# Spreading the attention weights one step earlier in a two-layer convolution block

## The chip, the cores and the metric

The kernel runs on one core of a Trainium2 chip. The metric is the device time of one execution in microseconds (us). Five engines of the core work side by side, each through its own queue in order: TensorE (PE, matrix products and transposes), VectorE (DVE, elementwise work and reductions), ScalarE (ACT, copies and activations), GpSimd (POOL, here it issues the gathers) and SyncE (SP, here it issues the plain transfers). Matrix products land in PSUM, from where ACT or DVE must fetch them before the place can be used again.

## The reference, cut to what matters

The input is 8 images of 256 channels and 64x64 positions, in float32. Two layers follow one another, each of the form x = x + layer(groupnorm(x)).

Layer 0 is attention over the 3x3 neighbourhood of each position, with 4 heads of 64 channels, together with a generated kernel:

```
q, k, v   = w_qkv @ x                        (1x1)
attn      = softmax over the 9 neighbours of q . k
kernel    = w_kg @ cat + b_kg                (9 values per head and position)
out       = w_proj @ (alpha * sum_k kernel * v_k + beta * sum_k attn * v_k)
```

Layer 1 is a modulated deformable 3x3 convolution: a small convolution gives 18 offsets and 9 masks per position, the image is sampled bilinearly at 9 moved places, and the samples are multiplied by a 256x256 matrix per tap and added.

## The kernel before, in words

**Tiling.** An image is cut into 8 chunks (`NC`) of 8 rows, that is 512 positions. 256 channels are 2 tiles of 128 partitions. In the attention, a chunk is seen as 8 tiles of 8x8 positions, each with a 10x10 neighbourhood of 100 keys (`NK`).

**Two streams.** The convolution of one image is woven into the attention of the next. The convolution is a loop over slots: one slot is one chunk and one of 9 taps, so 72 slots per image. A slot holds, on PE, 8 transposes of sampled rows (`pt`, line 816) and 8 passes of product matmuls (`po`, line 833). On ACT it holds two copies of the transposed rows (line 819) and four scalings of gathered rows (`s`, line 787), on DVE four times three multiply-adds (the sums, `s`, line 795), on POOL four gathers (`g`, line 771). The sums run 6 blocks of 128 positions ahead of the transposes, the scalings 8, the gathers 18; gathered rows have 10 buffers, and a slot has 4 blocks. The transposes use a PSUM pool of their own (`ps_t`), and so do the products (`ps_o`, one buffer, so that the first product of a chunk waits until DVE has added the chunk before to its residual, line 844).

**Front steps.** The attention of the next image, and after it the preparation of its convolution (table of rows, offsets, positions), is a generator, and each `yield` ends a step. The slot loop runs `transposes`, half of the look-ahead work, `product`, then a front step (a little over one per slot: there are 73 steps per image), then the other half of the look-ahead work. In a slot that ends a convolution chunk both halves and the final adds (`finished`) come before the front step. The order on PE, ACT, DVE and POOL is the order of the program text. The first image's front runs alone, before any slot.

**A chunk of attention** has seven steps. `a_` is the chunk itself, `d` the chunk before it, whose second half is worked off in between:

1. spread the weights of `d` (`spread_weights`), then `q` of `a_`
2. `k`
3. `products` q.k; `weighted(0)` of `d`
4. `logits`, second half of the value tiles of `d` (`keys(1)`), generated kernel, first part of the softmax
5. first half of `v`; `weighted(1)` of `d`; second part of the softmax; normalization of the next chunk
6. second half of `v`; first half of the output projection of `d` and its addition; `softmax_3`, which leaves the combined weights in `wts`
7. second half of the projection of `d`, its addition (`add`, line 544), statistics and storing of `d` (`second_stats`, line 548 and an SP transfer); `weights` (transposes of `wts`, line 467, copied to `wsb` by ACT, line 473); `keys(0)` (transposes of `v`, line 503, copied to `vk` by ACT, line 508)

After chunk 8 there are six more steps in which its second half is finished and the second group normalization is formed.

`spread_weights` does, per head, one matmul with a constant matrix of zeros and ones (line 480), which places the 9 weights of each position on its 100 keys, and one DVE product with a mask (line 488). Its four results live in the four buffers of `wk`.

**The shared PSUM pool.** All front steps take their PSUM from one pool in rotation, and a matmul waits until the user of the buffer four places earlier has been fetched:

```
ps_a = ctx.enter_context(tc.tile_pool(name="ps_a", bufs=4, space=PSUM))
```

In the kernel before, step 7 takes places for the projection, w and two vk; step 1 takes four for wk and two for q.

Of the kernel before, what the change touches and what calls it, by code (L numbers as in the profile page):

```python
# [19 lines left out]
NT = C // P  # L20
# [37 lines left out]
def preact_kernel(ctx: ExitStack, tc: tile.TileContext, a: dict, out: bass.AP):  # L58
# [161 lines left out]
    def normed(xt, gn, c):  # L220

        xn = xn2[c % 2]
        lo, hi = max(0, R * c - 1), min(H, R * c + R + 1)
        if c == 0:
            nc.vector.memset(xn[:, :, 0, :], 0.0)
        if c == NC - 1:
            nc.vector.memset(xn[:, :, R + 1, :], 0.0)
        o = lo - (R * c - 1)
        for ct in range(NT):
            nc.vector.tensor_scalar(  # L230
                xn[:, ct, o : o + hi - lo, 1 : W + 1],
                xt[:, ct, lo * W : hi * W].rearrange("p (r w) -> p r w", w=W),
                gn[:, 0, ct : ct + 1],
                gn[:, 1, ct : ct + 1],
                ALU.subtract,
                ALU.mult,
            )
        return xn
# [316 lines left out]
    def attention(b):  # L555

        xt = image
        gn = norm0[b]
        gn.means()
        stats = p2.tile([P, NT, NC, 6], F32, tag="stats", name=f"stats1_{b}")  # L560
        yield None
        gn = gn.ready()
        xn = normed(xt, gn, 0)
        yield None
        d = None
        for c in range(NC):
            a_ = Attention(b, c, xn, stats)
            if d:
                d.spread_weights()
            a_.q(0)  # L570
            a_.q(1)
            yield None
            a_.k(0)
            a_.k(1)
            yield None
            a_.products()
            if d:
                d.weighted(0)
            yield None
            a_.logits()  # L580
            if d:
                d.keys(1)
                d.carry_v()
            a_.generated()
            a_.softmax_1()
            a_.carry_k()
            yield None
            a_.v(0)
            if d:
                d.weighted(1)  # L590
            a_.turned()
            a_.softmax_2()
            if c + 1 < NC:
                xn = normed(xt, gn, c + 1)
            yield None
            a_.v(1)
            if d:
                d.add(0, d.project(0))
            a_.softmax_3()
            yield None  # L600
            if d:
                d.add(1, d.project(1))
                d.second_stats()
            a_.weights()
            a_.keys(0)
            yield None
            d = a_
        d.spread_weights()
        yield None
        d.weighted(0)  # L610
        d.keys(1)
        yield None
        d.weighted(1)
        yield None
        for m in range(NT):
            d.add(m, d.project(m))
        d.second_stats()
        gn = Norm(stats, f"1_{b}")
        yield None
        gn.means()  # L620
        yield None
        yield gn.ready()
# [129 lines left out]
    def fronts():  # L752
        for b in range(B):
            gn = None
            for got in attention(b):
                gn = got
                if gn is None:
                    yield
            yield
            yield from prepare(b, gn)  # L760
# [213 lines left out]
```

## Time and profile before

| what | value |
|---|---|
| time, median of 3 runs | 5197.73 us (5185.96 to 5206.68) |
| the profiled execution | 5546.8 us |
| its span, first to last instruction | 5545.0 us |
| mean granted PE clock in it | 0.939 of full speed |
| PE busy | 4874.6 us (88%) |
| DVE busy | 4170.6 us (75%) |
| POOL busy | 3287.5 us (59%) |
| ACT busy | 2368.6 us (43%) |

The profiled execution is longer than the unprofiled ones. A group of the profile names the line, the engine, the operation, what is written and read and how often; then busy time and mean nanoseconds of one; then the idle time of that engine just before these instructions, and what ended it. A wait reads as who waited, for whom, microseconds in total, how many times, and the longest. In the order of time a line begins with start and duration in microseconds; the idle time before it stands in brackets. A matmul in float32 appears as two passes, and the ends of matmuls are modelled: their distance from start to start is the better measure.

### The profile page before, as it was taken

What the parts mean: (1) busy time and instruction counts of PE and PEld (TensorE: products, weight loads), DVE (VectorE), ACT (ScalarE), POOL (GpSimd) and SP (SyncE); (2) the same over time, 40 slices, a digit from 0 to 9 for tenths busy, and PEclk for the clock granted to TensorE, in tenths of its full rate; (3) what the DMA queues carried; (4) which work ended last, traced back from release to release, by engine and by line L of the source; (5) the groups of instructions that cost most, each with busy time, mean ns of one, the idle gap of its engine ahead of it and who ended that gap; (6) DMA issues with size and microseconds to landing.
All of it is one profiled execution on the core that took longest, in us unless ns stands there. A gap on an engine that the chain in (4) does not pass through costs nothing. (4 is left out here: it accounts for less than half of the span.)

```text
span 5545.0 us, 79699 instructions
## 1 busy us (share of the span) xinstructions
PE 4874.6 (88%) x26592; PEld 2725.8 (49%) x26592; DVE 4170.6 (75%) x10071; ACT 2368.6 (43%) x5184; POOL 3287.5 (59%) x2310
## 2 busy tenths in 40 slices
PE   7979998899988998899988999989898899887677
PEld 4545554455544554455544555445554555443333
DVE  4567787788877787778878787878777777876666
ACT  2334444444444444444444444444444444443333
POOL 0036565666646666566656666566664666647776
PEclk9989999999999999999999999999999999998878
DMA  2067777777787777877787777877778677787777
GB/s 85 21 236 251 247 249 278 262 256 260 262 311 249 266 262 283 289 247 265 260 284 278 252 268 252 302 260 258 252 256 322 242 260 258 274 300 275 274 278 279
DMA packets 476840, 1422.60 MB, mean 257 GB/s; under 512 B 46910, under 2 KB 114750, under 8 KB 476300
## 3 DMA queue, kind: packets, MB, share of 16 engines
q0 software_dynamic: 331776, 1208.11, 61.9%
q1 hardware_dynamic: 141902, 204.27, 10.2%
q10 hardware_dynamic: 2750, 5.12, 0.3%
q8 instruction: 210, 3.44, 0.2%
q14 instruction: 202, 1.65, 0.1%
HBM read 1280.19 MB, written 137.13 MB: 256 GB/s over the span
## 5 line engine op out<-in xcount | busy, mean ns | idle before, releaser
L771 POOL DMA_INDIRECT g<-table,idx x2304 | 3284.9, 1426 | 2236.2 <-DVE s L795 585.5
L795 DVE SCALAR_TENSOR_TENSOR s<-g,wt,s 128x256 f32<-128x256 f32 x6912 | 2796.0, 478 | 566.5 <-ACT s L787 399.9
L833 PE MATMUL po<-vt,w_conv 128*128 128x512 f32 x4608 | 2187.8, 620 | 63.0 <-DVE r L844 37.4
L833 PEld LDWEIGHTS po<-vt,w_conv 128*128 128x128 f32 x4608 | 880.2, 202 | 965.9 <-issue 923.9
L787 ACT ACTIVATE s<-g,wt 128x256 f32<-128x256 f32 x2304 | 1068.5, 509 | 562.5 <-DMA g<-table,idx 464.7
L816 PE MATMUL pt<-ident,s 128*128 128x128 f32 x4608 | 725.0, 295 | 262.7 <-ACT vt L819 129.9
L816 PEld LDWEIGHTS pt<-ident,s 128*128 128x128 f32 x4608 | 547.4, 149 | 557.9 <-issue 184.4
L819 ACT COPY vt<-pt 128x512 f32<-128x512 f32 x1152 | 614.7, 584 | 423.3 <-PE pt L816 271.9
L281 PE MATMUL psq<-xn,w_qkvT 128*128 128x512 f32 x512 | 291.1, 720 | 113.2 <-DVE wk L488 108.4
L359 DVE TENSOR_TENSOR qk<-qk,near_k 128x400 f32<-128x400 f32 x256 | 129.8, 567 | 306.1 <-PE qk L351 165.2
L656 PE MATMUL om<-xn,w_off 128*32 128x512 f32 x2304 | 291.9, 604 | 7.7 <-DVE pos L689 7.4
L289 ACT COPY q<-psq 128x512 f32<-128x512 f32 x128 | 75.0, 586 | 483.7 <-PE psq L281 436.2
L313 PE MATMUL psk<-xn,w_qkvT 128*128 128x264 f32 (+1 forms) x1088 | 249.3, 382 | 10.9 <-ACT k L326 10.9
L313 PE MATMUL psv<-xn,w_qkvT 128*128 128x264 f32 (+1 forms) x1088 | 258.4, 382 | 0.0
L281 PEld LDWEIGHTS psq<-xn,w_qkvT 128*128 128x128 f32 x512 | 112.1, 229 | 290.6 <-DVE wk L488 161.1
L528 ACT COPY acc<-av 128x512 f32<-128x512 f32 x128 | 74.9, 585 | 414.4 <-PE av L521 320.8
L533 PE MATMUL proj<-acc,w_projT 128*128 128x512 f32 x512 | 239.8, 596 | 3.3 <-ACT s L787 2.7
L313 PEld LDWEIGHTS psv<-xn,w_qkvT 128*128 128x128 f32 x1088 | 199.9, 190 | 83.3 <-issue 46.4
L313 PEld LDWEIGHTS psk<-xn,w_qkvT 128*128 128x128 f32 x1088 | 202.3, 191 | 73.3 <-issue 20.2
L351 PE MATMUL qk<-k,q 64*64 64x100 f32 x4096 | 165.3, 260 | 78.5 <-issue 75.4
L351 PEld LDWEIGHTS qk<-k,q 64*64 64x64 f32 x4096 | 119.4, 136 | 155.0 <-issue 139.0
L335 ACT COPY v<-psv 128x320 f32<-128x320 f32 (+1 forms) x272 | 111.5, 417 | 187.3 <-PE psv L313 171.1
(89 smaller groups left out, 3375.0 us busy)
## 6 DMA issues: line engine op xcount, KB each, us to landing
table<-ts SPq DMA_DIRECT2D x384, 176.0 KB
g<-table,idx POOLq DMA_INDIRECT x2304
x<-in_x_dram SPq DMA_DIRECT2D x64, 512.0 KB
x<-x SPq DMA_DIRECT2D x64, 512.0 KB
r<-x SPq DMA_DIRECT2D x64, 512.0 KB
out_dram<-r SPq DMA_DIRECT2D x64, 512.0 KB
w_conv<-in_w_conv_dram ACTq DMA_DIRECT2D x1, 2304.0 KB
w_qkv<-in_w_qkv_dram ACTq DMA_DIRECT2D x2, 384.0 KB
```

Of the source, the lines that this page charges most:

```text
L281: nc.tensor.matmul(ps, w_qkvT[:, ct, m * P : (m + 1) * P], window(self.xn, ct, 4), start=(ct == 0), stop=(ct == NT - 1),)
L313: nc.tensor.matmul(ps[:, : (hi - lo) * WP], w_qkvT[:, ct, o : o + P], self.xn[:, ct, lo:hi, :], start=(ct == 0), stop=(ct == NT - 1),)
L351: nc.tensor.matmul(both[h][64 * t : 64 * t + 64, n : n + NK], self.qt[r, ct, o * T * T : (o + 1) * T * T], kt[r, ct, :, T * o : T * o + KT ...
L359: nc.vector.tensor_mul(qk[:, 2 * jj : 2 * jj + 2, :, h, :], both[h][:, : 4 * NK].rearrange("p (j c k) -> p j c k", j=2, c=NT), near_k.unsq ...
L533: nc.tensor.matmul(ps, w_projT[:, ct, m * P : (m + 1) * P], self.acc[:, ct].rearrange("p (t y x) -> p y t x", y=T, x=T), start=(ct == 0), ...
L656: nc.tensor.matmul(ps[32 * g : 32 * g + 32, :], w_off[:, ct, k, :], window(xn, ct, k), start=(n < 4), stop=(n >= KK * NT - 4),)
L771: nc.gpsimd.indirect_dma_start(out=g, out_offset=None, in_=tables[b % 2], in_offset=bass.IndirectOffsetOnAxis(ap=found[b, c][0][:, j, k : ...
L787: nc.scalar.activation(s, g[:, 0:C], AF.Copy, scale=w[:, 0:1])
L795: nc.vector.scalar_tensor_tensor(s, g[:, q * C : (q + 1) * C], w[:, q : q + 1], s, ALU.mult, ALU.add)
L816: nc.tensor.transpose(pt[ct][:, j, :], s[:, ct * P : (ct + 1) * P], ident)
L819: nc.scalar.copy(v[:, ct, :], pt[ct].rearrange("p b n -> p (b n)"))
L833: nc.tensor.matmul(po[:, m, :], w_conv[:, ct, k, m * P : (m + 1) * P], v[:, ct, :], start=(k == 0 and ct == 0), stop=(k == KK - 1 and ct = ...
```

## The change

The spreading of a chunk's weights moves from step 1 of the next chunk to step 7 of its own chunk. In step 7 `weights` and `keys(0)` move ahead of the projection's second half; then come the projection, its addition, the spreading, and the statistics of the chunk before. Behind chunk 8 the step that held only its spreading is gone, and the two halves of the last projection are two steps in place of one, so that the number of steps is the same.

```diff
         for c in range(NC):
             a_ = Attention(b, c, xn, stats)
-            if d:
-                d.spread_weights()
             a_.q(0)
             a_.q(1)
             yield None
...
             a_.softmax_3()
             yield None
+            a_.weights()
+            a_.keys(0)
             if d:
                 d.add(1, d.project(1))
+            a_.spread_weights()
+            if d:
                 d.second_stats()
-            a_.weights()
-            a_.keys(0)
             yield None
             d = a_
-        d.spread_weights()
-        yield None
         d.weighted(0)
         d.keys(1)
         yield None
         d.weighted(1)
         yield None
-        for m in range(NT):
-            d.add(m, d.project(m))
+        d.add(0, d.project(0))
+        yield None
+        d.add(1, d.project(1))
         d.second_stats()
         gn = Norm(stats, f"1_{b}")
         yield None
```

## The prediction

> **What bounds the kernel now.** I read the page first, then the waits of TensorE in one image (2373 to 2806 us, the fifth image's seven chunk boundaries), then busy time by stretch, then the order of time around one boundary.
>
> ```profile
> PE 4874.6 (88%) x26592; PEld 2725.8 (49%) x26592; DVE 4170.6 (75%) x10071; ACT 2368.6 (43%) x5184; POOL 3287.5 (59%) x2310
> ...
> L281 PE MATMUL psq<-xn,w_qkvT 128*128 128x512 f32 x512 | 291.1, 720 | 113.2 <-DVE wk L488 108.4
> ```
>
> TensorE (PE) is busiest. One group, the q matmuls, has 113.2 us of idle time before it, 108.4 of it ended by VectorE's (DVE's) wk products. PE's waits in the fifth image, with total, times and longest:
>
> ```profile
> PE psq L281 <- DVE wk L488: 16.2, 7, 5.8
> PE qk L351 <- issue: 7.4, 14, 1.0
> PE po L833 <- DVE r L844: 3.1, 1, 3.1
> PE pt L816 <- DVE s L795: 1.6, 6, 0.5
> ```
>
> This wait is the largest and comes once per boundary. Busy time by stretch (stretch, length, PE, weight loads, DVE, ACT, POOL, clock, DMA); three run from the projection of step 7 to the transposes after the next chunk's q, then a whole image, then the last image's convolution alone:
>
> ```profile
> 2559.60:2574.50 14.90, 12.49 (x49) 6.01 (x48) 14.90 (x35) 4.75 (x10) 11.25 (x6) 1.00 0.76 257
> 2498.10:2514.80 16.70, 14.22 (x50) 6.62 (x49) 15.56 (x36) 4.82 (x10) 13.36 (x8) 0.90 0.80 271
> 2434.20:2454.50 20.30, 14.31 (x49) 6.79 (x48) 19.00 (x44) 5.76 (x12) 16.06 (x8) 0.83 0.77 254
> 2373.00:2806.00 433.00, 401.48 (x2267) 232.55 (x2268) 343.75 (x795) 196.72 (x440) 278.34 (x195) 0.96 0.75 260
> 5010.00:5540.00 530.00, 382.82 (x1111) 191.15 (x1109) 341.70 (x834) 194.79 (x410) 376.46 (x268) 0.83 0.74 282
> ```
>
> Over the image PE is busy 401.48 of 433.00 us and DVE 343.75: PE bounds it. But inside the first stretch DVE is busy without a break: here DVE bounds, and PE waits on it. The order of time there:
>
> ```profile
> 2558.64 0.37 DVE L455 SCALAR_TENSOR_TENSOR wts<-lt,beta,kb 128x144 f32<-128x144 f32 x1
> 2558.93 4.83 DVE L795 SCALAR_TENSOR_TENSOR s<-g,wt,s 128x256 f32<-128x256 f32 x12
> 2559.59 1.88 PE L533 MATMUL proj<-acc,w_projT 128*128 128x512 f32 x4
> 2561.31 0.60 PE L467 MATMUL w<-ident,wts 128*128 128x128 f32 x4
> 2561.75 1.04 PE L503 MATMUL vk<-ident,v 128*100 128x128 f32 x8
> 2562.62 0.60 PE L816 MATMUL pt<-ident,s 128*128 128x128 f32 x4
> 2563.68 0.68 DVE L544 TENSOR_TENSOR x<-proj,x 128x512 f32<-128x512 f32 x1
> 2564.09 3.60 PE L833 MATMUL po<-vt,w_conv 128*128 128x512 f32 x8
> 2565.47 4.83 DVE L795 SCALAR_TENSOR_TENSOR s<-g,wt,s 128x256 f32<-128x256 f32 x12
> 2567.62 1.12 PE L480 MATMUL wk<-wsb,spread 9*100 9x512 f32 x8
> 2570.21 2.48 DVE L488 TENSOR_TENSOR wk<-wk,near 100x512 f32<-100x512 f32 x4
> 2570.95 3.71 PE L281 MATMUL psq<-xn,w_qkvT 128*128 128x512 f32 x8 [2.21 <-DVE wk L488]
> 2574.50 1.04 PE L816 MATMUL pt<-ident,s 128*128 128x128 f32 x8
> ```
>
> The four wk matmuls take all four buffers of the PSUM pool. DVE reaches their products only after twelve sums (4.83 us), and q, behind them on PE, needs the buffers back.
>
> [...] while q waits 2.21 us, transposes behind it, which need no PSUM of this pool, wait too. [...] with the same work and the same 2.21 us wait, the second stretch has clock 0.90 and lasts 16.70, not 14.90.
>
> **The change part by part.** No instruction is added or removed per chunk. The four wk matmuls (eight passes in the trace) and their four DVE products move one step up; in step 7 the order becomes w, vk, projection, add, wk, statistics.
>
> *A usual boundary (4 of 7 per image), timed from 2559.59.* PE distances from the start times above: projection 1.72, w 0.44, vk 0.87, one wk 1.12/4 = 0.28, q 3.55. After: w needs wts, which ends at 2559.01, 0.58 early; the projection no longer covers that, and nothing is lost while the margin lasts (up to 1.72 if it is gone). wsb's ACT copy is covered by vk and the projection. So w, vk, projection and three wk end at 0.44 + 0.87 + 1.72 + 0.84 = 3.87. The fourth wk takes the projection's buffer, so it waits for the add: this wait is new. The add is behind the sums, so it starts at 4.08 as now and ends at 4.76; with the fourth wk PE goes on at about 5.1. Queued behind it are the convolution's transposes, 0.9 (they are stretched to 1.47 by sums now; by 5.1 those are done), products 3.5, q 3.55: the next transposes start at 13.1 against 14.91 now. DVE: add until 4.7, wk products 2.4, statistics 1.2, twelve sums 4.75: 13.0, just in time for those transposes; the six sums (2.46) that now stand behind wk inside the stretch fall after it, where DVE has a 0.67 us wait today. Gain 1.8 at full clock. Slowed boundaries last 16.7 to 16.9; [...] I leave a third of the present loss. The four last 16.3 on average here, 15.4 in the calmer seventh image; 15.85 less 13.5 (13.1 plus 0.4) is 2.35, times 4 is 9.4 per image. Ends: 1.8 x 4 = 7.2 and 3 x 4 = 12.
>
> *The boundary at 2434 (one per image).* A convolution chunk is finished in the slot of q, so DVE does 18 sums and two adds of 0.64 before wk, and PE waits 5.78. After: add 4.7, wk 7.1, statistics 8.3, sums 15.4, adds 16.6; the convolution's next product, which needs those adds, starts at 16.7 against 21.2 now. Gain 4.5.
>
> *The first boundary* (no projection, wait 0.76): wk follows vk at 1.3 and hides DVE's lateness for the next transposes; 10.5 against 11.5, gain 1.0. *The sixth* (chunk finished in step 7, the add only at 7.7): the fourth wk waits until 8.5, transposes follow, and the end is where it was: 0, or a loss of 1 if the clock cools longer.
>
> *Sum:* 9.4 + 4.5 + 1.0 = 14.9 per image, times 7 interleaved images: 104.
>
> *Elsewhere.* The eighth chunk's step 7 grows by 1.5 (PE's next product at 6.0 for 4.5), the spread step behind it disappears (1.1), and the last add before the second normalization stands alone, about 1 less DVE time ahead of its matmul: taken as +0.6 per image, 4 in all, bounds -10 and +15. In the first image's front, with nothing interleaved, wk's products wait for the add: 0.4 x 7 = 3 lost. SP's store of the block, issued behind the statistics, goes 2.4 later; its reader is in a later image. SP is passed by nothing else. POOL: the twelve sums come later and free gather buffers later; below.
>
> Total 104 + 4 - 3 = 105. The profiled execution is 5546.8 us, 1.8 of it outside the span, so 5442. The unprofiled median, 5197.7, is 349 lower; the waits are made of DVE durations, which I take as unchanged, so I subtract the same 105: **5092 us**. Scaling by 5197.7/5546.8 would give 98 and 5099.
>
> **The rivals.** *DVE takes it all back.* It is full in the usual stretch. If all its present work must still fit ahead of the transposes, only its idle time there can be won. Over the seven stretches of the image that is 116.8 - 108.4 = 8.4, less 3.4 of the sixth: 5 per image, 35 in all: 5163. Against it: the last six sums are not needed by those transposes.
>
> *The gathers turn it slower.* The twelve sums end at 13.0 in place of 10.7 and free gather buffers 2.4 late; if POOL issues at once, data, ACT's scaling and DVE's sums come as much later. Fully exposed, 2.4 x 56 steps (8 per image) = 134, less 105: 5227. It decides once the gathers' slack is so small that over 105/56 = 1.9 per step comes through. For it: at 2443 and 2447 ACT does wait 2.58 and 3.71 for gathers. Against it: ACT's wait for gathers between 2446 and 2746 is small,
>
> ```profile
> ACT s L787 <- DMA g<-table,idx: 7.0, 3, 3.7
> ```
>
> and POOL issues the gather that reuses the first of these buffers at 2571.41, 3.5 after the first six sums ended (2567.9): it is behind anyway.
>
> *The clock gains more.* If no boundary cools any more, and c. 1 us more per boundary falls away after it: 12 + 5.5 + 1 + 1 per image, times 7, is 137; with the tail's +15, 152: 5046. For it: four of seven stretches here are slowed.
>
> *Nothing moves:* if PE's idle time only shifts to the new wait for the add, 5198. Against it: that wait is 0.9, not 2.2.
>
> **How the numbers follow.** Forecast 0.60 (own range 5060 to 5130), DVE 0.17, clock 0.10, slower 0.08, nothing 0.05. A measurement of this kernel tells about 0.5% (26 us) from no change. Faster: 0.60 + 0.10 + 0.13 of DVE's 0.17 = 0.83; same: 0.05 + 0.04 = 0.09; slower 0.08. The range takes in clock and most of DVE: 5035 to 5175.
>
> **What would show it.** Right: q's wait for wk near 0; a wait of about 0.9 at the fourth wk ended by the add; no wait of w for wts over 0.5; usual stretches near 13.1 to 13.5; the boundary that waits 5.78 now shorter by over 4 with a wait of the product for the two adds in its place; clock in these stretches nearer 1.00. Wrong: w waiting for wts, transposes waiting for sums by over 1 us, or ACT's wait for gathers (464.7 in all now) up by 50 or more.

## The result, and the profile after

The changed kernel takes 5218.51 us (median of 20 runs, 5200.66 to 5230.65) where the kernel before takes 5199.17 (20 runs, 5185.96 to 5219.39). The ratio is 1.0029, with a 95% interval of 1.0017 to 1.0042: 0.3% slower, which is less than the 0.5% that the prediction named as the least it could tell from no change. The forecast was 5092.

One thing must be known to read the numbers: both kernels take longer on some chips than on others, the kernel before some 5200 us on one kind and 5530 to 5560 on the other, and the profile shown ahead of the prediction (5546.8 us) fits the second. ("Kind of chip" is only a name for these two levels: each chip is on record in one session, so the cause may lie in the session and not in the chip.) The profile after (5205.54 us, span 5203.8) is of the first kind. So it is set beside a second profile of the kernel before on a chip of that kind (5206.58 us, span 5204.8); times are compared only within one kind, and kernels by their ratio to the kernel before on the same chip.

The page of the changed kernel, busy time by engine and the group of the q matmuls (line numbers from 567 on are one lower than before):

```profile
PE 4778.5 (92%) x26592; PEld 2668.8 (51%) x26592; DVE 4173.8 (80%) x10071; ACT 2379.9 (46%) x5184; POOL 3148.3 (60%) x2310
...
L281 PE MATMUL psq<-xn,w_qkvT 128*128 128x512 f32 x512 | 236.3, 604 | 1.6 <-DVE xn L230 1.6
```

The wait that the prediction set out to remove is gone: q had 113.2 us of idle time before it, and has 1.6. PE's waits in the fifth image (2376 to 2806 us) of the changed kernel, with total, times and longest:

```profile
PE wk L480 <- DVE x L544: 6.6, 6, 3.5
PE po L832 <- DVE r L843: 5.9, 3, 2.1
PE pt L815 <- ACT vt L818: 3.8, 1, 3.8
PE av L521 <- DVE qk L359: 3.6, 2, 2.0
```

In the place of q's wait stands the fourth wk's for the addition. The wait in the last line, which was 1.5 us in the fifth image of the first profile before, is not at a boundary. Busy time by stretch at the same boundaries, first of the kernel before (its second profile; stretch, length, PE, weight loads, DVE, ACT, POOL, clock, DMA; the first two end at the transposes behind q, the third at the product behind them):

```profile
2475.84:2490.75 14.91, 12.49 (x50) 6.02 (x49) 14.91 (x35) 4.75 (x10) 11.25 (x6) 1.00 0.75 250
2415.67:2432.26 16.59, 14.18 (x49) 6.62 (x48) 15.46 (x36) 4.75 (x10) 12.63 (x7) 0.90 0.78 257
2352.24:2374.54 22.30, 16.31 (x57) 7.99 (x56) 19.05 (x44) 6.35 (x13) 17.72 (x9) 0.77 0.77 259
```

and then of the changed kernel:

```profile
2478.36:2492.03 13.67, 13.08 (x50) 6.31 (x49) 13.67 (x32) 4.82 (x10) 8.27 (x5) 1.00 0.80 265
2419.43:2434.78 15.35, 14.76 (x50) 7.37 (x48) 15.35 (x36) 4.82 (x10) 9.95 (x5) 0.89 0.71 236
2359.79:2376.51 16.72, 14.11 (x57) 7.10 (x56) 16.72 (x39) 8.18 (x17) 11.02 (x6) 1.00 0.66 230
```

A usual boundary at full clock went from 14.91 to 13.67, a slowed one (clock 0.90 and 0.89) from 16.59 to 15.35, the long one from 22.30 to 16.72. Each of the three is shorter, and the time is not. Where the gain went can be read from a division of the whole span, worked out from the traces. A boundary runs from the first matmul of step 7 to the first product after the next chunk's q; seven boundaries and the seven stretches behind them make up most of an image; the values per image are means over the third to the eighth image.

| us | before, second profile | after, first profile | after, second profile |
|---|---|---|---|
| first slot begins (first image's front alone) | 359.7 | 382.9 | 385.5 |
| seven boundaries | 121.5 | 111.7 | 112.2 |
| seven stretches between them | 290.9 | 299.3 | 297.7 |
| step 7 of chunk 8 to the second normalization | 41.8 | 40.6 | 41.5 |
| from there to the next image's first boundary | 178.5 | 177.0 | 177.2 |
| slots of the seven interleaved images, sum | 4436.0 | 4413.5 | 4417.6 |
| the last image's convolution | 409.0 | 407.3 | 415.1 |

The boundaries gain 9.5 us per image, 66 in seven images. The stretches between them, in which the change touches no instruction, lose 7.6 (mean of the two profiles), 53 in seven. The first image's front, once per execution, loses 24.5. The first row and the last two add up to the span, which is 1.0 us shorter in the first and 13.4 us longer in the second of these profiles than before.

### The profile page after: what moved, and what is told of

Its sections match the earlier page's. It is cut to its first block, busy times and chain, and to the rows that moved or that the text cites. A ratio compares the mean times of both kernels' runs of the same rounds, so it can differ in the third digit from the quotient of the medians.

```text
span 5203.8 us, 79622 instructions
## 1 busy us (share of the span) xinstructions
PE 4778.5 (92%) x26592; PEld 2668.8 (51%) x26592; DVE 4173.8 (80%) x10071; ACT 2379.9 (46%) x5184; POOL 3148.3 (60%) x2310
## 5 line engine op out<-in xcount | busy, mean ns | idle before, releaser
L770 POOL DMA_INDIRECT g<-table,idx x2304 | 3145.7, 1365 | 2033.3 <-DVE s L794 757.7
L786 ACT ACTIVATE s<-g,wt 128x256 f32<-128x256 f32 x2304 | 1089.4, 510 | 637.3 <-DMA g<-table,idx 567.6
L832 PEld LDWEIGHTS po<-vt,w_conv 128*128 128x128 f32 x4608 | 866.9, 198 | 960.2 <-issue 882.5
L815 PE MATMUL pt<-ident,s 128*128 128x128 f32 x4608 | 685.1, 286 | 106.9 <-DVE s L794 82.1
L815 PEld LDWEIGHTS pt<-ident,s 128*128 128x128 f32 x4608 | 527.0, 145 | 425.0 <-issue 173.6
L281 PE MATMUL psq<-xn,w_qkvT 128*128 128x512 f32 x512 | 236.3, 604 | 1.6 <-DVE xn L230 1.6
L544 DVE TENSOR_TENSOR x<-proj,x 128x512 f32<-128x512 f32 x128 | 87.9, 687 | 133.2 <-PE proj L533 133.2
L480 PE MATMUL wk<-wsb,spread 9*100 9x512 f32 x512 | 146.5, 641 | 51.0 <-DVE x L544 50.5
L326 ACT COPY k<-psk 128x264 f32<-128x264 f32 (+1 forms) x272 | 97.4, 372 | 196.2 <-PE psk L313 196.1
```

What stands on the lines that cost most here:

```text
L281: nc.tensor.matmul(ps, w_qkvT[:, ct, m * P : (m + 1) * P], window(self.xn, ct, 4), start=(ct == 0), stop=(ct == NT - 1),)
L480: nc.tensor.matmul(ps[:NK], spread[32 * h : 32 * h + KK], self.wsb[32 * h : 32 * h + KK], start=True, stop=True,)
L770: nc.gpsimd.indirect_dma_start(out=g, out_offset=None, in_=tables[b % 2], in_offset=bass.IndirectOffsetOnAxis(ap=found[b, c][0][:, j, k : ...
L786: nc.scalar.activation(s, g[:, 0:C], AF.Copy, scale=w[:, 0:1])
L815: nc.tensor.transpose(pt[ct][:, j, :], s[:, ct * P : (ct + 1) * P], ident)
L832: nc.tensor.matmul(po[:, m, :], w_conv[:, ct, k, m * P : (m + 1) * P], v[:, ct, :], start=(k == 0 and ct == 0), stop=(k == KK - 1 and ct = ...
```

## The experiments

**A second profile of each kernel, on one chip.** No edit.

> The kernel before, unchanged, profiled a second time. The first profile of it lasted 5546.8 us, 6.7% over its own median of 5199; the profile of the changed kernel lasted 5205.5. If the first profile was disturbed (slower transfers from outside the kernel), this one lasts 5180 to 5230 and its last image, the convolution alone, takes about 410 us as in the changed kernel in place of 544; then the waits that the forecast was built on are to be read again from here. If profiling itself costs the kernel before 6%, it lasts 5500 or more again.

> The changed kernel, unchanged, profiled again beside the kernel before on one chip: 5200 to 5230. Theory A (the boundaries between chunks gain what was forecast and another stage gives it back): its seven boundaries per image sum to 8 to 15 us less than those of the kernel before, and the tail of each image's attention, its preparation or the last image is longer by as much. Theory B (the boundaries of an undisturbed kernel before had less to give): the boundaries differ by under 4 us per image and every stage by little.

Measured: 5206.58 and 5219.98 us, the table's first and third columns. Both losses named above are in the second profile of the changed kernel as they are in the first. The theory is from here on: the boundary works, and two other places pay for it. The rivals are that the numbers of the boundary are wrong, or that a single cause makes both losses.

**The first image's front in its old order.** In the first image nothing is interleaved, so the chain of work is bare. The order of time in one step 7 of it, the kernel before:

```profile
139.88 3.60 PE L533 MATMUL proj<-acc,w_projT 128*128 128x512 f32 x8
144.95 0.37 DVE L455 SCALAR_TENSOR_TENSOR wts<-lt,beta,kb 128x144 f32<-128x144 f32 x1
145.47 0.63 PE L467 MATMUL w<-ident,wts 128*128 128x128 f32 x4 [1.99 <-DVE wts L455]
148.78 3.71 PE L281 MATMUL psq<-xn,w_qkvT 128*128 128x512 f32 x8
```

and the changed kernel:

```profile
147.91 0.37 DVE L455 SCALAR_TENSOR_TENSOR wts<-lt,beta,kb 128x144 f32<-128x144 f32 x1
148.33 0.67 PE L467 MATMUL w<-ident,wts 128*128 128x128 f32 x4 [3.62 <-DVE wts L455]
148.83 1.88 PE L503 MATMUL vk<-ident,v 128*100 128x128 f32 x8
150.50 2.76 PE L533 MATMUL proj<-acc,w_projT 128*128 128x512 f32 x4
155.08 3.71 PE L281 MATMUL psq<-xn,w_qkvT 128*128 128x512 f32 x8
```

Before, both halves of the projection (eight passes) ran while the softmax was not yet ready, in time in which PE had nothing else; w then waited 1.99. After, PE waits 3.62, and the second half runs behind w and vk, on the path from `wts` to the next chunk's q. After that wait PE is slowed as well: from 148.9 to 152.2 the granted clock is 0.50, vk takes 1.88 and four projection passes 2.76, where they take 1.04 and 1.88 at full clock. From the start of `wts` to q it is 7.17 us for 3.83, and a chunk's period rises from 27.16 to 30.5 (from the third chunk on). The experiment gives the first image alone the old order:

```diff
         for c in range(NC):
             a_ = Attention(b, c, xn, stats)
+            if d and b == 0:
+                d.spread_weights()
...
-            a_.weights()
-            a_.keys(0)
+            if b > 0:
+                a_.weights()
+                a_.keys(0)
             if d:
                 d.add(1, d.project(1))
-            a_.spread_weights()
+            if b > 0:
+                a_.spread_weights()
             if d:
                 d.second_stats()
+            if b == 0:
+                a_.weights()
+                a_.keys(0)
             yield None
             d = a_
+        if b == 0:
+            d.spread_weights()
```

> The changed kernel, with the first image's attention, which runs alone, in the order of the kernel before; the seven interleaved images keep the change. If the first image lost by the order of step 7 (the projection no longer runs while PE waits for the softmax weights, 1.6 us a chunk, and the clock cools in the longer wait), the first slot starts at 360 us in place of 384 and the time is 20 to 26 lower: 5190 to 5200. If the later start came from something else (the start of the program), 5210 to 5225.

Measured: 5192.99 us (5183.8 to 5216.81), ratio to the kernel before 0.9994 (0.9981 to 1.0007). The first slot begins at 360.4 us, as before the change, and the median falls by 25.5 us (by the two ratios it is 0.35%, some 18 us), near the 24.5 that the table showed. This loss is separate from the other, which is left as it was: seven stretches between boundaries take 296.8 us per image in it.

**What fills the stretches between the boundaries.** In the changed kernel a stretch with a loss looks like this, in the order of time behind one boundary:

```profile
4428.69 11.95 DVE L794 SCALAR_TENSOR_TENSOR s<-g,wt,s 128x256 f32<-128x256 f32 x30
4431.48 9.97 POOL L770 DMA_INDIRECT g<-table,idx  x1 [2.35 <-DVE s L794]
...
4444.56 0.51 ACT L786 ACTIVATE s<-g,wt 128x256 f32<-128x256 f32 x1 [2.03 <-DMA g<-table,idx]
4445.10 0.48 DVE L794 SCALAR_TENSOR_TENSOR s<-g,wt,s 128x256 f32<-128x256 f32 x1 [4.47 <-ACT s L786]
...
4449.80 2.01 DVE L359 TENSOR_TENSOR qk<-qk,near_k 128x400 f32<-128x400 f32 x4
4450.42 1.01 PEld L521 LDWEIGHTS av<-wk,vk 100*64 100x64 f32 x32 [2.63 <-DVE qk L359]
4450.42 1.15 PE L521 MATMUL av<-wk,vk 100*64 100x64 f32 x32 [2.44 <-DVE qk L359]
```

VectorE does thirty corner sums without a break, 11.95 us. GpSimd starts a gather 2.8 us into them and is not done with it until 9.97 us later, 0.8 after the last sum, where an ordinary gather takes 0.94. The next gathers are late by as much; so are ACT's scalings, DVE's sums, DVE's product for q.k that is queued behind these, and PE. Elsewhere it is k's copy on ACT that stands behind a scaling, and PE's q.k that waits for it: 21.9 us, five times, in the whole profile. Before the change the wk products, whose second operand lies in PSUM, stood between twelve of these sums and the eighteen behind them, and in places a wait of DVE for ACT; 4 unbroken runs of thirty sums are in that trace, and 21 after the change (20 in its second profile); none is longer. In both kernels most gathers of over 1.5 us end 0.8 us after a run of sums (357 of 360 before, 304 of 312 after), so gathers were held before, too, and the time lost in long ones is even a little less after (898 us for 931). But more of them are held very long: over 8 us last 14 before and 22 after (23 in the second profile), and it is one of these behind which PE waits above. To begin inside a run is not enough: of 853 gathers of the changed kernel that begin inside a run with over 1 us of it still to go, 300 are held.

The hold is of some 23 sums, from 4431.48 to the end of the run at 4440.64, and not of one of 0.48 us.

Four experiments take this apart. The first two put a memset of one column (59 ns, 1152 times) ahead of each group of sums, in the changed kernel and in the kernel before. It runs while a sum does, so that DVE's busy time grows by only 9 us (4182.6 for 4173.8 in the changed kernel):

```diff
         work = [sums[n] for n in (i, i + 1) if n in sums]
+        if work:
+            nc.vector.memset(pause, 0.0)
         for q in range(1, 4):
```

> The changed kernel with one more VectorE instruction in front of every group of six (or three) sums: it sets one column of a tile that nothing reads. Theory A (a gather that POOL issues while VectorE runs sums without a break is held until the run ends; the change joined 12 and 18 sums to 30): runs of sums are 6 long at most, no gather lasts over 3.5 us, ACT's wait for gathers falls from 568 us to under 450, the stretches between the boundaries go back from 298 to about 291 us per image; less some 0.1 us for each of 1152 groups where VectorE bounds, 5160 to 5200 us. Theory B (VectorE is full and simply late, whatever POOL does): the added instructions make it later still, 5225 to 5300.

> The kernel before with the same added instruction. Theory A: it too has gathers held by runs of 12 and 18 sums (931 us over the 0.94 us of a free one); they fall below 300 us, but its transposes seldom wait for gathers, so the time moves little: 5180 to 5215. Theory B: slower by the added work, 5210 to 5280.

Measured on one chip: 5073.03 us (5069.23 to 5077.91), ratio 0.9747 (0.9721 to 0.9774), for the changed kernel; 5103.71 (5102.34 to 5104.84), ratio 0.9809 (0.9782 to 0.9835), for the kernel before. An instruction added on the second busiest engine made both kernels faster, and by more than the theory had it (5160 to 5200 and 5180 to 5215). In the changed kernel with the memset, the order of time at a place like the one above:

```profile
4328.72 0.06 DVE L795 MEMSET pause<- 128x1 f32 x1
4329.11 2.46 DVE L798 SCALAR_TENSOR_TENSOR s<-g,wt,s 128x256 f32<-128x256 f32 x6
4331.11 0.06 DVE L795 MEMSET pause<- 128x1 f32 x1
4331.49 2.46 DVE L798 SCALAR_TENSOR_TENSOR s<-g,wt,s 128x256 f32<-128x256 f32 x6
4331.50 0.94 POOL L772 DMA_INDIRECT g<-table,idx  x1 [4.01 <-DVE pause L795]
```

The gather again starts 2.8 us behind the first sum (at 4328.71) and just after the start of a sum, and takes 0.94. No gather of the 2304 lasts over 1.25 us. The gathers' group in the changed kernel,

```profile
L770 POOL DMA_INDIRECT g<-table,idx x2304 | 3145.7, 1365 | 2033.3 <-DVE s L794 757.7 <-DVE pi L691 359.3 <-ACT s L786 272.4
```

and with the memset:

```profile
L772 POOL DMA_INDIRECT g<-table,idx x2304 | 2329.0, 1011 | 2721.1 <-DVE pause L795 913.3 <-ACT s L788 367.5 <-DVE gt L697 367.2
```

(busy time and mean ns; then the idle time, which is no loss by itself). ACT's waits for gathers go from this in the changed kernel

```profile
ACT s L786 <- DMA g<-table,idx: 567.6, 473, 9.0
```

to this with the memset:

```profile
ACT s L788 <- DMA g<-table,idx: 238.9, 271, 5.6
```

With the hold taken away from both kernels, the loss between the boundaries is gone, and the change gains again:

| us | before + memset | after + memset |
|---|---|---|
| first slot begins | 358.9 | 390.5 |
| seven boundaries, per image | 124.5 | 112.4 |
| seven stretches between them, per image | 290.9 | 291.3 |
| step 7 of chunk 8 to the next image's first boundary | 205.2 | 208.2 |
| slots of the seven interleaved images, sum | 4346.9 | 4289.1 |
| the last image's convolution | 395.9 | 396.4 |

The interleaved images are 57.8 us shorter with the change, of which the first image's front takes 31.6 back. Much of what the memset itself brings lies elsewhere: from step 7 of chunk 8 to the next image's first boundary it takes the kernel before from 220 to 205 us per image and the changed kernel from 218 to 208. In the kernel before it takes nothing from the stretches, and its boundaries are 3 us per image longer with it.

The third puts the statistics of the chunk before, which the change had moved to the end of step 7, at the start of the next step, in front of q:

```diff
-        d = None
+        d = old = None
         for c in range(NC):
             a_ = Attention(b, c, xn, stats)
+            if old:
+                old.second_stats()
             a_.q(0)
...
             a_.spread_weights()
-            if d:
-                d.second_stats()
             yield None
-            d = a_
+            old, d = d, a_
+        old.second_stats()
         d.weighted(0)
```

> The changed kernel with the two statistics of a chunk moved from step 7 to the beginning of the next step 1, so that they stand between 12 and 18 sums: no work added or taken away. Theory A: no run of 30 sums is left at the boundaries, the longest gathers there last 5 to 7 us in place of 10, the stretches between boundaries lose 3 to 6 of their added 7 us per image: 5175 to 5205. Theory B: VectorE has as much to do in the same time, 5210 to 5225.

Measured: 5182.0 us (5171.6 to 5190.52), ratio 0.9956 (0.9941 to 0.9972). The statistics (1.27 us) now stand between the twelve sums and the eighteen behind them: 3 unbroken runs of thirty in place of 21, 9 gathers of over 8 us in place of 22, and the stretches between boundaries take 292.8 us per image in place of 298.5. No work is added or taken away in it, and the memset's other effects play no part; but the order of DVE's work changes too, and what that is worth by itself is seen further down ("The mends together"). The first image's loss stays (387.6).

The fourth asks whether the break must be an instruction without two SBUF inputs (Theory A1), as the memset and the wk products with their operand in PSUM are, or can be any small one (A2). It puts an addition of two small SBUF tiles (two columns) in the memset's place:

```diff
+        if work:
+            nc.vector.tensor_add(pause, pair[0], pair[1])
```

> The changed kernel with another small instruction at the same places: a sum of two two-column tiles, both in SBUF, in place of the one-column set without an input. Theory A1 [...]: gathers stay held, some still last 10 us, ACT's wait for gathers stays over 450 us, 5200 to 5260 us. Theory A2 (any small instruction that interrupts the sums lets POOL in, by its short time or by a pause of the engine): as with the set, no gather over 3.5 us and 5070 to 5110 us.

Measured on a chip of the second kind: 5375.41 us (5367.76 to 5390.54), ratio 0.9732 (0.9701 to 0.9763). No gather is over 2.3 us long, but 510 are over 1.5. Of the gathers that begin inside a group of six with over 1 us of it still to go, 209 of 786 are held, all until 0.8 us after the end of their group. So a hold ends where the unbroken run of the large sums ends, and a short instruction with two SBUF inputs ends it, too. The memset does more: on a chip of that kind none of 842 gathers that begin in the same way inside a group is held, so that it keeps holds from beginning and does not only end them. Why is not settled by this. Nor is which gathers are caught: in the changed kernel 298 of the 300 held ones begin within 52 ns behind the start of a sum, with the addition none of the 209.

**The projection ahead of the weights.** Step 7 with the projection first, as in the kernel before, and the spreading still in step 7:

```diff
-            a_.weights()
-            a_.keys(0)
             if d:
                 d.add(1, d.project(1))
+            a_.weights()
+            a_.keys(0)
             a_.spread_weights()
```

> The changed kernel with the projection and its addition ahead of the weights' transposes in step 7, as the kernel before had them; the spreading stays in step 7. The projection covers the wait for the softmax weights again in the first image: the first slot starts at 360 to 368 us in place of 384. But the first of the four spreading matmuls now takes the projection's PSUM buffer, so all four wait for the addition, not only the last: some 0.8 us more at the usual boundaries, 20 to 35 us in all. Together 5190 to 5230 us.

Measured on a chip of the second kind: 5665.75 us (5652.36 to 5672.21), ratio 1.0240 (1.0209 to 1.0271). The first slot begins at 358.0 us, so the first image's loss comes from the place of the projection and not from that of the spreading. The boundaries are as short as in the changed kernel on such a chip (112.5 us per image for 113.2), so the 0.8 us that each was to lose did not come. But it was 2.4% slower than the kernel before, and nothing in the theory so far made so much.

**The mends together.** The memset with the old order of the first image; then these two with the statistics moved as above for all images but the first:

> The changed kernel with both mends together: the added one-column instruction ahead of each group of sums (alone 5073 us), and the first image in the old order (alone 25 us less than the changed kernel). If the two losses are separate, they add: 5040 to 5055 us, first slot at 360 to 365 us.

> The kernel with both mends, and the statistics moved from step 7 to the next step 1 in the interleaved images. With the runs of sums broken in any case, the move can only bring the sums 1.2 us earlier after step 7 and the statistics later: no gain from gathers is left, -1.2 us at the boundaries where VectorE ends last (the one at which a chunk of the convolution is finished), so 0 to 15 us less than both mends alone. If the gain of 36 us that this move brought alone came from VectorE's order and not from the gathers, it brings 25 to 40 here too.

Measured on a chip of the second kind, beside a kernel before of 5527.94 us: 5268.24 (5252.59 to 5291.71), ratio 0.9534 (0.9507 to 0.9561), and 5205.58 (5204.82 to 5223.9), ratio 0.9429 (0.9403 to 0.9454). The first slots begin at 361.3 and 359.4 us, as expected. But moving the statistics took off 63 us, more than the 0 to 15 of the theory and than the 25 to 40 of its rival, and no gather is held in either kernel. 57 of them are in the interleaved images, 17 in the stretches between the boundaries (306.8 and 304.4 us per image). So the order of DVE's work is worth something by itself, at least here, and the gain of the third experiment can't be put down to the gathers alone. The second is the fastest version found, by ratio; it wasn't run on a chip of the first kind.

**The changed kernel where the kernel before takes 5530.** It had not been seen there, so it was run beside the mended version:

> The changed kernel as it is, beside a kernel that has all three mends, on one chip. Theory (the change gains some 9 us an image at its boundaries and gives 7 to 8 back through gathers held by joined sums, and 25 in the first image): ratio to the kernel before 0.998 to 1.006, whatever the level of the chip. Rival (what the change loses depends on the chip): where the kernel before takes some 5500 us the ratio leaves that band, by over 0.5% in either direction.

> The changed kernel with a one-column memset ahead of each group of corner sums, the first image's lone front in its old order, and the statistics at the start of the next step. Theory: the three mends act on different stretches and add up; from 5073.0 of the kernel with the memset alone, 25 less in the first image and up to 20 less between the boundaries give 5030 to 5050 where the kernel before takes 5200, a ratio of 0.967 to 0.971; where the kernel before takes 5530 the ratio is 0.943 again, and the changed kernel beside it stays within 0.6% of the kernel before. Rival (the statistics gain only while gathers are held): 5045 to 5055 and a ratio of 0.970 to 0.972.

Measured on a chip of the second kind: 5694.08 us (5688.01 to 5702.03), ratio 1.0295 (1.0275 to 1.0314), for the changed kernel; 5208.05 (5207.09 to 5215.82), ratio 0.9424 (0.9406 to 0.9441), for the mended one. For the changed kernel the rival was right: what the change costs depends on the chip, and here it is 3%. PE's waits show an item that was small on the first kind,

```profile
PE qk L351 <- issue: 192.8, 294, 2.5
```

and the order of time shows its form, in a place where a gather of some 10 us has just ended and the others follow one upon the other:

```profile
2613.32 1.28 PE L351 MATMUL qk<-k,q 64*64 64x100 f32 x43
2613.79 0.94 POOL L770 DMA_INDIRECT g<-table,idx  x1 [0.30 <-issue]
...
2617.18 0.40 PE L351 MATMUL qk<-k,q 64*64 64x100 f32 x1 [1.14 <-issue]
2617.62 0.94 POOL L770 DMA_INDIRECT g<-table,idx  x1 [0.30 <-issue]
2618.59 0.32 PE L351 MATMUL qk<-k,q 64*64 64x100 f32 x1 [1.01 <-issue]
```

The 64 small matmuls of q.k come one by one, up to 1.4 us apart, with nothing shown that they wait for. Such a group takes 1.66 us on average in the kernel before at the first level (1.70 in the changed one), 3.81 in the profile shown ahead of the prediction, and 6.56 here. Within this execution it takes 1.8 us where the DMA engines are under 60% busy (8 groups), 8.0 where they are over 90% busy (48), and 12.3 where a gather of over 8 us ended just before (15). The difference to the kernel before, 2.75 us on 64 groups, is 176 us, where the kernel as a whole loses 167 and the stretches between the boundaries 215 (31 per image, as the table below has it). The kernel with the projection first has the same groups (6.59 us) and is 0.5% nearer to the kernel before, by its better front. Busy DMA engines alone don't do it: at the first level the group takes 1.64 with DMA over 90% busy (some 35 groups of the kernel before).

What stayed open was whether these bursts come from the held gathers, or the new order of PE costs this by itself there. The pair of kernels with the memset tells it, on a chip of the second kind:

> The kernel before with a one-column memset ahead of each group of corner sums. Where the kernel before takes some 5530 us: theory (the changed kernel loses 3% there because a held gather is followed by a burst of gathers during which TensorE's q.k products are issued late; without held gathers there is no burst): ratio 0.955 to 0.970, and the 64 q.k stages last 2.4 to 3.2 us on average in place of 3.8. Rival (the loss there comes from the new order of TensorE itself): 0.98, as where it takes 5200. Where it takes 5200: 0.981 again.

> The changed kernel with the same memset, beside it. Theory: it is the faster of the two on either kind of chip, by 0.4 to 0.8% (31 us where the kernel before takes 5200); where that takes 5530, ratio 0.955 to 0.965 and q.k stages of 2.4 to 3.2 us. Rival (the new order of TensorE costs by itself where the kernel before takes 5530): the slower of the two there, by 1% or more.

Measured beside a kernel before of 5562.5 us: 5352.23 (5347.06 to 5356.05), ratio 0.9623 (0.9604 to 0.9643), without the change; 5327.4 (5312.28 to 5340.02), ratio 0.9567 (0.9541 to 0.9593), with it. Once no gather is held, the change gains 25 us here too, although its first front loses 32. Worked out from the traces at this level:

| us | before | after | before + memset | after + memset |
|---|---|---|---|---|
| seven boundaries, per image | 121.3 | 113.2 | 124.0 | 113.5 |
| seven stretches between them, per image | 310.6 | 341.3 | 305.3 | 310.2 |
| one group of q.k | 3.81 | 6.56 | 2.51 | 2.74 |

(the first column is the profile of 5546.8 us). The boundaries gain 8 to 12 us per image on either kind of chip. The loss of 31 us per image between them shrinks to 5 when the gathers are not held. The kernel with the addition agrees by another instruction: with holds of at most some 2 us its stretches take 313.7 us per image and a group of q.k 4.00. Shown is that the loss goes when the long holds go, with either instruction; why PE's issue is so late on some chips is not shown by anything here.

## Why the prediction was wrong

Three steps failed. The new place of the sums was taken as free, and the interleaved images lost 53 us between their boundaries. The first image's front was put at 3 us and lost 24.5. And the wk matmuls were priced too low, so that with a smaller gain in clock the boundaries gave 66 us and not 104.

**The boundaries: right in kind, two thirds in size.** Forecast was 14.9 us per image, measured 9.8 (9.2 in the second profile), 66 for 104.

- *The usual boundary.* At full clock 13.1 was forecast and 13.67 measured. The term that was off is the wk matmuls. They were priced by their starts, 0.28 each, and PE was to go on 0.3 after the add. In the profile after:

```profile
4423.54 1.11 PE L480 MATMUL wk<-wsb,spread 9*100 9x512 f32 x6
4424.50 0.68 DVE L544 TENSOR_TENSOR x<-proj,x 128x512 f32<-128x512 f32 x1
4425.24 1.10 PE L480 MATMUL wk<-wsb,spread 9*100 9x512 f32 x2 [0.59 <-DVE x L544]
4426.27 1.09 PE L815 MATMUL pt<-ident,s 128*128 128x128 f32 x8
```

From the fourth wk to the transposes behind it are 1.03 us. In the kernel before, the four stand together: their first passes start within 0.02 us and their second passes 0.5 later, and where transposes follow at once, these start 1.05 after the first of the four. So four cost as much as one, and the change, which parts the fourth from the others, pays twice. The wait of the fourth wk for the add is 0.59 there (0.9 was the sign named). On the first boundary, q's wait of 0.76 was for one wk product (0.69 us), which DVE began as soon as the matmuls had ended: DVE was not late there, and this boundary gained 0.4 and not 1.0.
- *The clock.* It was to lose two thirds of its cost, which was the author's estimate. In the profile ahead of the prediction, q behind a wait of 2.21 us takes 5.40 at a granted clock of 0.69 (from 2509.5 to 2515.0), and behind an equal wait 3.71 at 1.00 (from 2570.95 to 2574.50): what sets the clock at a boundary is not shown by the length of this wait. Over seven boundaries, the time lost to a clock below full went from 11.1 to 8.8 us per image. So the four usual boundaries gained 1.53 each on average, 6.1 and not 9.4.
- *The long boundary.* Forecast 4.5 and a product that starts at 16.7; measured 5.1 and 16.72 (the mean of six images). Right.
- *The sixth.* Forecast 0, at worst a loss of 1; measured a loss of 1.9, with the fourth wk waiting some 3.5 us.

**The first image's front: the step that failed by a factor of eight.** The prediction counted only waiting for the add, 0.4 us seven times. Its own sentence on the usual boundary named the danger: the projection no longer covers w's wait for `wts`, which costs nothing while the margin lasts. With no convolution between, there is no margin, and DVE's softmax bounds: PE had spent its wait on the projection. Measured: 24.5 us.

**Between the boundaries: the step that was taken as free.** The forecast moved six sums out of the stretch to a place "where DVE has a 0.67 us wait today", and took that as free. That wait, and the wk products ahead of it, were what ended the run of sums. The sum over DVE's time was right; what the order of these instructions does to another engine was not asked. The gathers' rival had the right engine and the wrong reason: buffers set free 2.4 us late, 134 us if fully exposed. What came was gathers held by a run of thirty sums, 53 us, on the first kind of chip; that its 5227 lies near the measured 5218.51 is luck. The sign that it named did come: ACT's wait for gathers rose from 524.1 to 567.6, or by 103 against the 464.7 that the prediction had.

**The end of the front.** +4 was forecast with bounds of -10 and +15; step 7 of chunk 8 and what follows it to the next image gain 2.2 us per image, 15 in seven: at the upper bound.

Together on the first kind of chip: 66 + 15 gained, 53 + 24.5 lost, a gain of 4 where the medians show a loss of 19. The terms are means over six images of two executions, whose spans differ by 14.4 us themselves; the remaining 20 us or so (0.4%) are not assigned.

**The base.** That the waits at the boundaries are alike in the two kinds of execution was right (121.3 and 121.5 us). But the profile had a line whose weight was not asked for, PE's q.k waiting for "issue", 7.4 us in one image. It was the trace of a chip on which held gathers cost far more; there the change costs 167 us; the only case of the prediction on that side, with a chance of 0.08, had 29.

## What to carry to other kernels

A wait that ends on a full engine can be moved away, but ask of each instruction that leaves its place what it separated: here four products (2.48 us) had parted twelve sums from eighteen, and in a joined run of thirty (11.95 us) a gather on GpSimd was held from 2.8 us after its start to 0.8 us after its end (9.97 us for 0.94). Where a fill, a prologue or a tail runs without its usual companion, cost the new order there by itself, along the chain that bounds it, and not as a share of the usual stretch. When VectorE runs groups of sums like these (128x256, 0.48 us each) beside GpSimd gathers, try a tiny instruction between the groups: here a memset of 59 ns, 1152 times, added 9 us to VectorE's busy time on the first kind of chip and made both kernels faster, by 1.9 and 2.5% on one kind of chip and by 3.8 and 4.3% on the other.

## What the runs showed of the hardware

- A gather that begins inside a run of corner sums can last until 0.8 us after its end, up to 9.97 us in the changed kernel, where most take 0.94. With a 59 ns memset ahead of each group of six sums none is held (the longest takes 1.25 us on the first kind of chip), not even of those that begin inside a group (842 with over 1 us of it to go, on the second kind). A small addition with two SBUF inputs in its place lets a hold last to the end of the group, so that no gather takes over 2.3 us. Of the gathers that begin inside a run, only a part is held (300 of 853 in the changed kernel).
- The kernel before takes 6 to 7% longer on some chips than on others. Of some 340 us, 138 lie in small matmuls that PE issues late for no reason that the profile shows, and 135 in the last image's convolution, which has none of them (544 us for 409): the group of 64 q.k matmuls takes 1.66 us in the kernel before on one kind of chip, 3.81 in the slower execution, and 6.56 in the changed kernel there; without held gathers it is 2.5 to 2.7. One and the same change so costs 0.3% on one chip and 3% on another.
- Four matmuls that contract over nine rows each, at rows 0, 32, 64 and 96, start within 0.02 us, and other work follows 1.05 us after the first of them. One of them that comes alone takes 1.03. The mean distance between starts, 0.14 per pass, is no price.
